# The last three rotations of the front and the first three local units in one hand-written order, with attention's buffers at the other end of SBUF

## The chip, the core and the metric

The kernel runs on one core of a Trainium2 chip. The metric is the device time of one execution in microseconds (us). One execution is also taken by the hardware profiler; the profile's times count from the first instruction of the program.

The engines are named as the profile names them: PE (TensorE, matmuls; PEld is its weight load), DVE (VectorE), ACT (ScalarE), POOL (GpSimd) and SP (SyncE, which here only issues DMAs). Each runs its own instructions in order, and they wait for each other by semaphores.

## The reference, cut to what matters

The input `x` is [16, 128, 128]: 16 samples of 128 tokens with 128 features. Two levels are computed; the change lies at the seam inside the first one.

```python
x = x + attn(cond(x))                    # level 0: conditioned 16-head causal attention
x = x + ffn(rigid_transform(x))          # level 0: each sample is rotated and moved as an image,
                                         #   then 6 layers of local attention + gated feed-forward
x = x + gated_linear_attention(laplace(x))   # level 1
x = x + moe(...)                             # level 1

def rigid_transform(X):   # per sample: bilinear samples of the 128x128 image at turned positions
    return sum of 4 gathers of X at (iy, ix), weighted by the distances

def local_layer(x):       # 6 times
    q, k, v = split(shift(x) @ Wqkv)                     # 16 heads of 64
    q, k = rotary(l2norm(q) * qs), rotary(l2norm(k) * ksc)
    x = softmax(band(q @ k.T)) @ v @ Wo + x
    return gated_gelu_ffn(layernorm(shift(x))) + x
```

## The kernel before, in words

**Stages.** `stage_front` does attention and rotation, `stage_local` the six local layers, `stage_tail` level 1. Inside a stage the order of PE, DVE, ACT and POOL is written out by hand: `run_step` walks a list such as `t.scores(0) w.rows(0) ...` and calls each piece in turn, and `manual_schedule` keeps that order on the four engines. SP's DMAs are placed by the tile framework's own scheduler. A letter stands for an object: `w` is the rotation (`Warp`) of one sample.

**The front.** `FRONT_STEP` is run for n = 0 to 18. In step n, attention of sample n begins (`t`), that of sample n-1 ends (`o`), and the rotation of sample n-3 is done (`w`). So step 16 ends attention of sample 15 and rotates sample 13; steps 17 and 18 only rotate samples 14 and 15. `o.write()` stores the attended sample as an image in DRAM, from which `gather` (POOL, eight indirect DMAs a sample) fetches boxes of pixels. A rotation then makes, on four quarters t: `far` (ACT, L479 and L486, distances), `hat` (DVE, L494, one SBUF tile clipped in place, two a quarter), `spread` (DVE, L455, `diag` from `box` and `own`, both in SBUF, two a sample), `rows` (PE, L502), `times` (DVE, L510, `prod` from PSUM and a hat), `sums` (PE, L520), and at the end `keep` (ACT, L527, and SP's `fr_moved` and `xs` DMAs), which puts the moved sample into `xs`.

**The local layers.** `Local` opens its pools after all of the front's pools are closed, so its weights lie over the front's buffers. `Layer(lo, 0)` loads `wqkv` (1536 KB), `wo` (512 KB), three pieces of `w2` (170 KB), `w1` (341 KB) and small tables; `prepare` makes `tab` (POOL, L673), `b1n` (PE L678, then DVE L684) and `w1n` (POOL, L686). Layer 1's weights are loaded right behind.

`STEP` is run for groups of four samples n = 0, 4, 8, ... In it `p0` to `p3` are the four new units: `project` (PE, L706, four a unit), `square` (ACT, L711), `cossin` (DVE, L719, `t`, four a unit), `sum_squares` (DVE, L729, two a unit), `rotate` (POOL, L743, four a unit), `lengths` (POOL, L735 and L736, the `pow`), `normalize_keys` (POOL, L748). `t0` to `t3` are units two behind, `o0` to `o3` three behind: `transpose` (PE, L770), `scores` (PE, L787), `mask` (DVE, L794), `maxima` (DVE, L801 and L806), `exponentials` (ACT, L814), `normalize` (POOL, L822), `turn`, `weigh`, `out`. So the group n = 0 has `p0` to `p3`, `t2` and `t3` (samples 0 and 1) and `o3` (sample 0) only. `f`, `e`, `g`, `h` are the feed-forward of earlier groups.

**The seam to the tail.** After the last feed-forward (`hT`, L941; `add`, DVE L955 into `xs`), `stage_local` turns the samples back on PE (L1019) and adds them to `xres` (DVE, L1025). `Tail` opens its pools over the local ones, clears `aT` (POOL, L1173), and `laplace` begins with `lx` (POOL, L1226; DVE, L1237), `diffuse` goes on with L1249, L1253 and L1256.

Of the kernel before, what the change touches and what calls it, by code (L numbers as in the profile page):

```python
# [15 lines left out]
P = 128  # L16
# [37 lines left out]
class Front:  # L54


    def __init__(self, s, ctx, xres):
        self.s, self.tc, self.nc, self.xres = s, s.tc, s.nc, xres
        tc, nc, a = s.tc, s.nc, s.a
        self.pools = {  # L60
            n: ctx.enter_context(tc.tile_pool(name=f"fr_{n}", bufs=n)) for n in (1, 2, 3, 4, 6)
        }
        self.sm = ctx.enter_context(tc.tile_pool(name="fr_sm", bufs=6))
        psum = lambda name, n: ctx.enter_context(
            tc.tile_pool(name=name, bufs=n, space=bass.MemoryType.PSUM)
        )
        self.rings = {"w": (psum("fr_w", 3), 1024), "g": (psum("fr_g", 2), 512)}
        self.n = 0
        self.image = [
            tc.dram_tile([P // 2, 13, 2, 32], F32, name=f"fr_image{b}") for b in range(B)  # L70
        ]
        self.moved = tc.dram_tile([B, P, 256], F32, name="fr_moved")
        wp = self.pools[1]
        by = lambda name, shape, src, eng=None: load(s, wp, name, shape, src, eng)


        self.tok = by("tok", [P, B], a["tok7"])
        self.wqk = [[None, None], [None, None]]
        for h in range(2):
            for k in range(2):  # L80
                self.wqk[k][h] = by(
                    f"wqk{k}{h}", [P, 512], a["a0_wqk"][k][:, 512 * h : 512 * h + 512], nc.scalar
                )
        self.cbias = by("cbias", [8, P], a["c0_bias"])

        self.xT = self.tile(1, "xT", [P, B, P])
        nc.sync.dma_start(out=self.xT[:, 0:4], in_=a["xT"][:, 0:4])
        self.bqk = by("bqk", [P, 2, 8], a["a0_bqk"])
        self.move = by("move", [P, 3, B], a["moves"])


        self.corner = by("corner", [P, 2, EIGHTS + QUADS], a["k_corner"])
        self.lane = by("lane", [P, 2], a["k_lane"])
        self.late = by("late", [P, 1024], a["k_late"])
        self.wv = by("wv", [P, 1024], a["a0_wv"], nc.scalar)
        nc.sync.dma_start(out=self.xT[:, 4:B], in_=a["xT"][:, 4:B])
        self.wo = by("wo", [P, 8, P], a["a0_wo"].rearrange("(c p) e -> p c e", p=P), nc.scalar)
        self.bv = by("bv", [P, 8], a["a0_bv"])
        self.bo = by("bo", [P, P], a["a0_bo"])
        nc.sync.dma_start(out=xres, in_=a["x"].rearrange("b t f -> t b f"))  # L100

        self.own = by("own", [P, 4], a["k_own"])
        self.sel = by("sel", [P, 44], a["k_quad"])

        self.eps = self.tile(1, "eps", [P, 1])
        nc.gpsimd.memset(self.eps, EPS_MASK)
        self.rem = self.tile(1, "rem", [P, 16])
        nc.gpsimd.iota(
            self.rem, pattern=[[1, 16]], base=0, channel_multiplier=0,
            allow_small_or_imprecise_dtypes=True,  # L110
        )
# [3 lines left out]

    def ps(self, ring):

        self.n += 1
        pool, cols = self.rings[ring]
        return pool.tile([P, cols], F32, tag=ring, name=f"{ring}{self.n}")  # L120

    def rows(self):

        nc, s = self.nc, self.s
        tokf = self.tile(1, "tokf", [P, B])
        nc.vector.tensor_copy(tokf, self.tok)
        self.row = self.tile(1, "rows", [P, B], U32)
        nc.vector.tensor_scalar(self.row, tokf, 128.0, s.pidx[:, 0:1], ALU.mult, ALU.add)
        self.onehot = self.tile(1, "onehot", [8, B])
        nc.vector.tensor_scalar(self.onehot, tokf[0:8], s.pidx[0:8, 0:1], None, ALU.is_equal)  # L130

    def lean(self):
        pb = self.ps("g")
        self.nc.tensor.matmul(pb[:, 0:B], self.cbias, self.onehot, start=True, stop=True)
        self.lean_of = self.tile(1, "lean", [P, B])
        self.nc.vector.tensor_copy(self.lean_of, pb[:, 0:B])
# [7 lines left out]
    def whole(self):  # L144


        pc = self.ps("g")
        for c in range(8):
            self.nc.tensor.matmul(
                pc[:, 0:P], self.bv[:, c : c + 1].to_broadcast([P, P]), self.wo[:, c, :],  # L150
                start=(c == 0), stop=(c == 7),
            )
        self.bias = self.tile(1, "bias", [P, P])
        self.nc.vector.tensor_tensor(self.bias, pc[:, 0:P], self.bo, ALU.add)
# [86 lines left out]
class Condition:  # L241
# [5 lines left out]
    def fetch(self):  # L247
        self.w = self.fr.tile(6, "wcond", [P, P])
        self.nc.gpsimd.indirect_dma_start(
            out=self.w, out_offset=None, in_=self.fr.s.a["c0_wT"],  # L250
            in_offset=bass.IndirectOffsetOnAxis(ap=self.fr.row[:, self.b : self.b + 1], axis=0),
            bounds_check=8 * P - 1,
        )

    def condition(self):
# [3 lines left out]
        if not self.pair:  # L259
            self.pair.append(self.fr.tile(3, "y", [P, 2, P]))  # L260
# [10 lines left out]
class Half:  # L271
# [17 lines left out]
    def keep(self, j):  # L289
        k, pr = j % 2, 4 * self.half + j // 2 * 2  # L290
        if k not in self.T:
            self.T[k] = self.fr.tile(2, f"qkT{k}", [P, 8, 256])
# [14 lines left out]
class FirstUnit:  # L307
# [14 lines left out]
    def keep_values(self, c):  # L322
        if c == 0:
            self.v = self.fr.tile(2, "v", [P, 1024])
# [27 lines left out]
    def exponentials(self, half):  # L352
        sc3 = self.sc[half].rearrange("p (h k) -> p h k", h=8)
        self.pe[half] = self.fr.tile(3, "pe", [P, 8, P])
# [19 lines left out]
    def keep_turn(self, i):  # L374
        self.pT[i] = self.fr.tile(4, "pT", [P, 4, P])
# [16 lines left out]
    def keep_weighed(self):  # L392
        self.oT = self.fr.tile(2, "oT", [P, 8, P])
# [177 lines left out]
def stage_front(s, xres):  # L571
# [3 lines left out]
    with ExitStack() as ctx:  # L575
        fr = Front(s, ctx, xres)
# [7 lines left out]
        engines = {e.engine for e in (nc.tensor, nc.vector, nc.scalar, nc.gpsimd)}  # L584
        with s.tc.manual_schedule(engines=engines):
# [5 lines left out]
            for n in range(B + 3):  # L591
                at = {k: v[n + d] for k, (v, d) in lists.items() if 0 <= n + d < B}
                run_step(FRONT_STEP, at)
# [15 lines left out]
class Local:  # L609


    def __init__(self, s, ctx):
        self.s, self.tc, self.nc, self.a = s, s.tc, s.nc, s.a
        nc = self.nc
        self.pools = {
            n: ctx.enter_context(s.tc.tile_pool(name=f"lo_{n}", bufs=n)) for n in (1, 2, 4, 6)
        }
        self.sm = ctx.enter_context(s.tc.tile_pool(name="lo_sm", bufs=6))
        psum = lambda name, n: ctx.enter_context(
            s.tc.tile_pool(name=name, bufs=n, space=bass.MemoryType.PSUM)  # L620
        )
        self.rings = {"s": (psum("lo_s", 2), 1024), "g": (psum("lo_g", 4), 512)}
        self.n = 0
# [4 lines left out]
        self.rot = load(s, self.pools[1], "rot", [P, 4, 64], self.a["k_rot"])  # L628
        self.band = load(s, self.pools[1], "band", [P, P], self.a["k_band"])
        self.mean = self.tile(1, "mean", [P, P])  # L630
        nc.vector.memset(self.mean, 1.0 / P)
        self.power = self.tile(1, "power", [P, 32])
        nc.vector.memset(self.power, -0.5)
        self.xs = s.xs
# [4 lines left out]
    def ps(self, ring):  # L639

        self.n += 1
# [9 lines left out]
class Layer:  # L651


    def __init__(self, lo, L):
        self.lo, self.number = lo, L
        s, nc, a, two, one = lo.s, lo.nc, lo.a, lo.pools[2], lo.pools[1]
# [4 lines left out]
        self.w2 = lo.tile(2, "w2", [P, 3, P])  # L661
# [8 lines left out]
    def prepare(self):  # L670
        lo, nc = self.lo, self.lo.nc
        self.tab = lo.tile(2, "tab", [P, 4, 64])
# [10 lines left out]
        self.b1 = lo.tile(2, "b1n", [P, 6])  # L683
        nc.vector.tensor_tensor(self.b1, pb[:, 0:6], self.rawb, ALU.add)  # L684
        self.w1 = lo.tile(2, "w1n", [P, 682])
# [3 lines left out]
class Unit:  # L689
# [18 lines left out]
    def square(self, k, c):  # L708
        if ("sq", k) not in self.bank:
            self.bank["sq", k] = self.lo.tile(2, "sq", [P, 1024])  # L710
# [4 lines left out]
    def cossin(self, k, c):  # L715

        if k not in self.t:
            self.t[k] = self.lo.tile(2, "t", [P, 2, 16, 64])
# [19 lines left out]
    def rotate(self, k):  # L738
        t = self.t[k]
        self.rot[k] = self.lo.tile(6, "rot", [P, 16, 64])  # L740
# [265 lines left out]
def stage_local(s, xres, early):  # L1006

    nc = s.nc
    with ExitStack() as ctx:
        lo = Local(s, ctx)  # L1010
        engines = {e.engine for e in (nc.tensor, nc.vector, nc.scalar, nc.gpsimd)}
        with s.tc.manual_schedule(engines=engines):
            run_layers(lo, early)

        for b0 in range(0, B, 4):
            pt = lo.ps("s")
            for i in range(4):
                for k, (rows, x) in enumerate(lo.halves(b0 + i, 1)):
                    nc.tensor.transpose(  # L1019
                        pt[:, 512 * k + 64 * i : 512 * k + 64 * i + 64],  # L1020
                        x.rearrange("p i t -> p (i t)"), s.ident[rows, rows],
                    )
            for k in range(2):
                xg = xres[:, b0 : b0 + 4, 64 * k : 64 * k + 64]
                nc.vector.tensor_tensor(  # L1025
                    xg, pt[:, 512 * k : 512 * k + 256].rearrange("p (i f) -> p i f", i=4), xg,
                    ALU.add,
                )


def run_layers(lo, early):
    total = DEPTH * B
    layers, units, ffs = [Layer(lo, 0)], {}, {}
    layers[0].prepare()
    for n in range(0, total + 12, 4):
        L, b = divmod(n, B)
        if n < total:
# [4 lines left out]
            for i in range(4):  # L1042
                units[n + i] = Unit(lo, layers[L], b + i)
# [6 lines left out]
        run_step(STEP, at)  # L1050
# [671 lines left out]
def tile_rec_block(ctx: ExitStack, tc: tile.TileContext, a: dict, out: bass.AP):  # L1722
# [5 lines left out]
    with tc.tile_pool(name="xs", bufs=1) as pool:  # L1728
# [4 lines left out]
        stage_front(s, xres)  # L1733
        stage_local(s, xres, early)
# [142 lines left out]
```

## Time and profile before

| | us |
|---|---|
| three runs, median (lowest to highest) | 2581.92 (2580.78 to 2582.80) |
| the profiled execution, its own time | 2586.6 |
| its span, first to last instruction | 2584.8 |
| PE busy in the span | 2432.3 (94%) |
| DVE busy | 2211.7 (86%) |
| ACT busy | 1924.3 (74%) |
| POOL busy | 1995.0 (77%) |

The stages, by the first or last instructions that mark them: the last copy L527 of front step 15 starts at 397.4, those of steps 16, 17 and 18 at 418.0, 434.5 and 447.9; the first local projection starts at 465.5, the second group's (n = 4) at 519.7, the third's (n = 8) at 588.2; a group in the middle takes 71.4. The tail runs from about 2258 to 2584.8.

How to read it: the page gives busy time of each engine and the chain of work that ended last; the windows view gives busy time, the granted TensorE clock (PEclk, 1.00 is full speed) and the DMA rate of any stretch; the timeline gives each instruction with its start, its length and, in brackets, how long its engine was idle before it and what ended that. Times come from one profiled execution.

### The profile page before, as it was taken

The page shows a single profiled execution, that of the slowest core. Times are in us where ns is not written, and L with a number is a line of the kernel's source. Part 1 is how long each engine was busy: PE and PEld are TensorE (multiplying, and loading weights), DVE is VectorE, ACT ScalarE, POOL GpSimd, SP SyncE. Part 2 cuts the span into 40 slices and gives each one's busy share as a digit, 9 for nine tenths or more (in the row PEclk, how much of TensorE's full clock was granted, in tenths as well). Part 3 has the DMA queues.
Part 4 walks back from the last instruction along what each step waited for, and adds up shares of the span by engine and source line. Part 5 has one row for each costly group of instructions (what it writes and reads, how often), then busy time and mean ns, then how long its engine had stood idle before and what let it go on. Part 6 is the DMA issues. An engine that isn't in the chain of part 4 may idle for free. (4 is left out here: it accounts for less than half of the span.)

```text
span 2584.8 us, 47593 instructions
## 1 busy us (share of the span) xinstructions
PE 2432.3 (94%) x17644; PEld 1677.5 (65%) x17644; DVE 2211.7 (86%) x2961; ACT 1924.3 (74%) x5717; POOL 1995.0 (77%) x1242
## 2 busy tenths in 40 slices
PE   7999997699999989999999999999999999789998
PEld 5676765366666666666666666666667666456666
DVE  5899997699999989999899989999899998454544
ACT  4788886488888878888788878888788888443422
POOL 3777675799999989999999999999999999243210
PEclk9999999799999999999999999999999999889999
DMA  3111111200001000100001000100000000021220
GB/s 107 29 30 33 29 29 39 80 1 5 13 5 38 8 8 5 38 8 5 13 5 38 8 7 7 38 8 5 6 5 5 5 3 4 17 64 64 93 70 25
DMA packets 89487, 64.73 MB, mean 25 GB/s; under 512 B 56802, under 2 KB 75944, under 8 KB 88488
## 3 DMA queue, kind: packets, MB, share of 16 engines
q1 hardware_dynamic: 78280, 37.56, 5.8%
q0 software_dynamic: 9216, 22.03, 2.8%
q8 instruction: 140, 2.29, 0.4%
q10 hardware_dynamic: 1760, 2.10, 0.3%
q14 instruction: 91, 0.75, 0.1%
HBM read 55.06 MB, written 6.60 MB: 24 GB/s over the span
## 5 line engine op out<-in xcount | busy, mean ns | idle before, releaser
L814 ACT ACTIVATE pe<-s,nm,r 128x128 f32<-128x128 f32 x1536 | 682.7, 486 | 2.3 <-DVE nm L806 1.7
L736 POOL TENSOR_TENSOR r<-ss,power 128x32 f32<-128x32 f32 x96 | 543.3, 5659 | 8.0
L719 DVE TENSOR_TENSOR t<-g,tab 128x1024 f32<-128x1024 f32 x384 | 461.8, 1216 | 48.2 <-PE g L706 32.1
L743 POOL TENSOR_TENSOR rot<-t 128x512 f32<-128x512 f32 x384 | 480.5, 1274 | 28.7 <-DVE t L719 28.6
L822 POOL TENSOR_TENSOR pe<-pe,den 128x1024 f32<-128x1024 f32 x192 | 363.5, 1898 | 40.0 <-DVE den L821 38.7
L706 PE MATMUL g<-wqkv,xs 128*128 128x512 f32 x768 | 393.4, 613 | 0.8 <-DVE t L719 0.4
L814 ACT ACTIVATION_READ_ACCUMULATOR pe<-s,nm,r 128x1 f32 x1536 | 359.3, 234 | 0.0
L711 ACT ACTIVATE sq<-g 128x512 f32<-128x512 f32 x384 | 230.8, 608 | 132.0 <-PE g L706 93.6
L775 ACT COPY qkT<-g 128x512 f32<-128x512 f32 x384 | 220.3, 615 | 56.4 <-PE g L770 55.7
L770 PEld LDWEIGHTS g<-ident,rot 128*128 128x128 f32 x1536 | 176.8, 144 | 115.5 <-issue 43.0
L770 PE MATMUL g<-ident,rot 128*128 128x128 f32 x1536 | 228.5, 282 | 23.6 <-ACT qkT L775 9.1
L794 DVE TENSOR_TENSOR s<-s,band 128x1024 f32<-128x1024 f32 x192 | 234.7, 1223 | 12.6 <-PE s L787 12.1
L828 PEld LDWEIGHTS g<-ident,pe 128*128 128x128 f32 x1536 | 179.3, 141 | 99.8 <-issue 87.9
L729 DVE TENSOR_REDUCE ss<-sq 128x16 f32<-128x1024 f32 x192 | 231.6, 1207 | 3.0 <-ACT sq L711 1.0
L801 DVE TENSOR_REDUCE nm<-s 128x8 f32<-128x1024 f32 x192 | 233.0, 1213 | 0.9
L787 PE MATMUL s<-qkT,qkT 64*128 64x128 f32 x3072 | 224.0, 285 | 5.5 <-ACT qkT L775 5.5
L787 PEld LDWEIGHTS s<-qkT,qkT 64*128 64x128 f32 x3072 | 187.2, 188 | 62.2 <-issue 51.1
L828 PE MATMUL g<-ident,pe 128*128 128x128 f32 x1536 | 222.6, 275 | 0.8 <-POOL pe L822 0.7
L835 DVE COPY pT<-g 128x512 f32<-128x512 f32 x288 | 192.7, 683 | 17.5 <-PE g L828 13.5
L842 PE MATMUL g<-pT,v 128*64 128x128 f32 x3072 | 200.6, 278 | 2.0 <-DVE pT L835 2.0
L755 PE MATMUL g<-wqkv,xs 128*128 128x512 f32 x384 | 202.2, 608 | 0.0
L842 PEld LDWEIGHTS g<-pT,v 128*64 128x64 f32 x3072 | 165.4, 137 | 50.6 <-DVE nm L801 18.2
(333 smaller groups left out, 4784.5 us busy)
## 6 DMA issues: line engine op xcount, KB each, us to landing
wqkv<-in_lo_wqkv_dram SPq DMA_DIRECT2D x6, 1536.0 KB
roots<-lo_roots SPq DMA_DIRECT2D x24, 256.0 KB
fr_image<-xres SPq DMA_DIRECT2D x32, 104.0 KB
wo<-in_lo_wo_dram SPq DMA_DIRECT2D x6, 512.0 KB
box<-fr_image,idx POOLq DMA_INDIRECT x128
fr_moved<-out SPq DMA_DIRECT2D x16, 128.0 KB
w<-in_lo_w_dram SPq DMA_DIRECT2D x6, 341.0 KB
wqk<-in_a_wqk_dram ACTq DMA_DIRECT2D x4, 256.0 KB
```

Of the source, the lines that this page charges most:

```text
L706: self.nc.tensor.matmul(pq, self.xT, self.w.qkv[:, at : at + 512], start=True, stop=True)
L719: self.nc.vector.tensor_tensor(self.t[k][:, :, 8 * c : 8 * c + 8, :], heads(self.bank["q", k, c]).unsqueeze(1).to_broadcast([P, 2, 8, 64]) ...
L736: self.nc.gpsimd.tensor_tensor(self.r, self.ss, self.lo.power, ALU.pow)
L743: self.nc.gpsimd.tensor_tensor(self.rot[k][:, :, at], t[:, 0, :, at], t[:, 1, :, other], ALU.add)
L770: self.nc.tensor.transpose(pt[:, j * P : j * P + P], flat[:, at : at + P], self.s.ident)
L787: self.nc.tensor.matmul(sc[:, k * 512 + j * P : k * 512 + j * P + P], self.T[0][rows, pr, :], self.T[1][rows, pr, :], start=True, stop=True,)
L794: self.nc.vector.tensor_tensor(sc, sc, self.lo.band.unsqueeze(1).to_broadcast([P, 8, P]), ALU.add)
L801: nc.vector.tensor_reduce(nm, self.sc[half].rearrange("p (h k) -> p h k", h=8), AX.X, ALU.max, negate=True)
L814: self.nc.scalar.activation(self.pe[half][:, h, :], sc3[:, h, :], AF.Exp, bias=self.nm[half][:, h : h + 1], scale=self.r[:, hd : hd + 1], ...
L822: self.nc.gpsimd.tensor_tensor(pe, pe, den.unsqueeze(2).to_broadcast([P, 8, P]), ALU.mult)
L828: self.nc.tensor.transpose(pt[:, j * P : j * P + P], self.pe[i // 2][:, 4 * (i % 2) + j, :], self.s.ident)
L842: self.nc.tensor.matmul(po[rows, j * P : (j + 1) * P], self.v[:, hd * 64 : hd * 64 + 64], self.pT[2 * half + k][:, j, :], start=True, stop ...
```

## The change

1. **Two sides of SBUF.** Attention's buffers (its weights, `xT`, `y`, `qkT`, `v`, `pe`, `pT`, `oT`, small ones) go into pools `at_*` on the right end; what the rotations need stays in `fr_*` on the left. The `at_*` pools are closed after step 16's `o.write()`, by `FRONT_LAST`, which is `FRONT_STEP` cut there.
2. **Local's weights and the p-units' tiles on the right.** `Local` opens `2w`, `1w`, `2p`, `6p` and `lo_sm` on the right as soon as attention's pools are closed, with `reuse_waits="tile"`: a tile waits for the tiles that lay at its addresses. The rest (`lo_1`, `lo_2`, `lo_4`, PSUM) is opened by `open()` once the front's pools are closed.
3. **One order for the seam.** `lo.begin()` loads layer 0's weights and runs `prepare`; then `BLEND` holds the rest of step 16 (`u`, sample 13), steps 17 and 18 (`v`, `w`, samples 14 and 15) and the units `p0`, `p1`, `p2`. Their projections take PSUM from the front's ring `w` (three buffers of two banks), half of a buffer each. `FIRST` takes the place of `STEP` for n = 0, without `p0` to `p2`.

```diff
 class Front:
-    def __init__(self, s, ctx, xres):
+    def __init__(self, s, ctx, ctx_at, xres):
+        self.at_pools = {
+            n: ctx_at.enter_context(tc.tile_pool(name=f"at_{n}", bufs=n, side="right"))
+            for n in (1, 2, 3, 4, 6)
+        }
...
+FRONT_LAST = FRONT_STEP[: FRONT_STEP.index("o.write()") + 1]
+BLEND = """
+u.rows(3) v.hat(0,0) v.far(0,1) u.times(2) v.gather(3) v.spread(0) u.sums(1) v.far(1,0)
+u.times(3) v.hat(1,0) v.rows(0) u.sums(2) v.far(0,2) v.hat(0,1) v.hat(0,2) v.rows(1) v.times(0)
+v.far(1,1) w.bases() v.hat(1,1) v.spread(1) v.far(0,3) p0.project(0,0) v.sums(0) v.far(1,2)
+v.hat(1,2) v.rows(2) v.times(1) w.far(0,0) p0.square(0,0) u.sums(3) p0.project(1,0) v.hat(0,3)
+p0.cossin(0,0) v.far(1,3) w.far(1,0) v.hat(1,3) v.times(2) p0.project(0,1) v.rows(3) w.gather(0)
...
+w.sums(3) p1.lengths() p2.cossin(0,0) p1.normalize_keys() w.keep() p2.square(0,1)
+p2.sum_squares(0) p2.cossin(0,1) p2.rotate(1) p2.rotate(0) p2.lengths() p2.normalize_keys()
+""".split()
...
-            for n in range(B + 3):
+            for n in range(B + 1):
                 at = {k: v[n + d] for k, (v, d) in lists.items() if 0 <= n + d < B}
-                run_step(FRONT_STEP, at)
+                run_step(FRONT_STEP if n < B else FRONT_LAST, at)
+    lo = Local(s, ctx_local, fr)
+    with s.tc.manual_schedule(engines=engines):
+        lo.begin()
+        at = dict(zip("uvw", warps[B - 3 :]))
+        run_step(BLEND, {**at, **{f"p{i}": lo.units[i] for i in range(3)}})
+    return lo
...
 class Local:
+    def begin(self):
+        s, nc = self.s, self.nc
+        self.layers.append(Layer(self, 0))
...
+        self.layers[0].prepare()
+        for b in range(4):
+            self.units[b] = Unit(self, self.layers[0], b)
+
+    def open(self):
+        pool = lambda name, n, **kw: self.ctx.enter_context(
+            self.s.tc.tile_pool(name=name, bufs=n, reuse_waits="tile", **kw)
+        )
+        for n in (1, 2, 4):
+            self.pools[n] = pool(f"lo_{n}", n)
...
     def ps(self, ring):
+        if self.rings is None:
+            return self.front.ps("w")[:, 0:512]
...
+FIRST = """
+t2.transpose(1,0) t2.transpose(0,0) t2.values(0) t2.keep_transpose(0,0) t2.keep_transpose(1,0)
...
+t3.normalize(1) p3.lengths() p3.normalize_keys()
+""".split()
...
-        run_step(STEP, at)
+        run_step(STEP if n else FIRST, at)
...
-        stage_front(s, xres)
-        stage_local(s, xres, early)
+        with ExitStack() as local:
+            with ExitStack() as front:
+                lo = stage_front(s, xres, front, local)
+            stage_local(s, lo, xres, early)
```

In the changed kernel as it is built, `prepare` is the first work after step 16's `o.write()` on PE, DVE and POOL, ahead of all of `BLEND`; on SP the load of `wqkv` waits for the last matmul of sample 15's `o.out()` and stands ahead of that sample's image; layer 1's loads stand directly behind layer 0's. From the group n = 4 to the last local group the four engines' orders are those of before. At the seam to the tail, DVE and POOL have `lx` of the first two tail groups ahead of the last feed-forward's `add` and of the clearing of `aT`.

## The prediction

> **What bounds the kernel now.** I read the page first. Its chain that ended last covers only the tail, so it says nothing of the seam between front and local layers. I therefore asked for busy time by stage (length, then busy us of PE, PEld, DVE, ACT, POOL, granted clock, DMA share, GB/s):
>
> ```profile
> 397.40:418.00 20.60, 17.79 (x160) 13.07 (x160) 15.90 (x19) 13.12 (x27) 16.18 (x14) 0.92 0.21 37
> 418.00:434.50 16.50, 11.54 (x96) 8.66 (x96) 13.95 (x15) 12.02 (x26) 10.69 (x10) 0.90 0.13 27
> 434.50:448.00 13.50, 9.86 (x96) 7.17 (x96) 11.09 (x13) 8.87 (x20) 0.00 (x0) 1.00 0.08 16
> 448.00:465.50 17.50, 2.25 (x12) 2.28 (x13) 0.27 (x3) 0.30 (x1) 2.75 (x2) 0.61 0.85 275
> 465.50:519.70 54.20, 40.83 (x206) 23.99 (x206) 42.68 (x45) 29.51 (x90) 45.89 (x27) 0.81 0.08 22
> 662.50:734.00 71.50, 70.79 (x526) 48.38 (x525) 67.57 (x83) 60.01 (x184) 66.82 (x38) 1.00 0.05 12
> ```
>
> The last line is the steady local layer: PE 70.8 of 71.5, so PE sets the pace and whatever is won before it stays won. At the seam nothing is full. From 397.4 to 519.7 are 122.3 us, in which DVE, the busiest, has 83.9 of work: at most 38 us can be won. The 17.5 us from 448.0 are a stop of all engines while DMA moves 275 GB/s. The timeline there shows the chain:
>
> ```profile
> 409.40 2.05 PE L399 MATMUL g<-wo,oT 128*128 128x128 f32 x16 [0.52 <-ACT oT L394]
> ...
> 453.14 0.55 SPq L1060 DMA_DIRECT2D wqkv<-in_lo_wqkv_dram  x1
> ...
> 462.65 2.02 POOL L686 TENSOR_SCALAR w1n<-w,gbb 128x682 f32<-128x682 f32 x1 [8.74 <-DMA gbb<-in_lo_gbb_dram]
> 463.25 2.41 PE L678 MATMUL g<-gbb,w 128*128 128x1 f32 x12 [15.40 <-DMA gbb<-in_lo_gbb_dram]
> 465.75 0.17 DVE L684 TENSOR_TENSOR b1n<-g,b 128x6 f32<-128x6 f32 x1 [17.32 <-PE g L678]
> ```
>
> The weights' load, then `prepare`, then the first projection. The first `cossin` is at 467.7; DVE stood from 448.3.
>
> **A. The load is moved, and its wait with it.** Now `wqkv` waits for the end of L399 (411.45); I take its issue at 411.9, where before the image store was issued. But `prepare` stands ahead of `BLEND` on PE (L678), DVE (`b1n`) and POOL (`tab`, `w1n`), so these three wait for `w1`, `gbb`, `scl` and `rot`; behind them wait all rotations, and POOL's gathers of samples 14 and 15. Before, 9.5 us passed from the issue of `wqkv` to `w1n`, with 2218 KB (`wqkv`, `wo`, `w2`) ahead of `gbb`. Now `w1` (341 KB) and the image (208 KB) are ahead too: 549 KB at 275 GB/s, 2.0 us. So L678 starts at 411.9 + 11.5 = 423.4 and DVE is free 2.41 + 0.17 + 0.1 later, at 426.1. Bounds: 9.5 us (424.1) and twice that, as the small loads on SP now each wait for an earlier landing (433.6). DVE, which reaches `b1n` at 413.5, stands 12.6 us where it stood 19.4. Layer 1's loads follow on SP and share the DMA engines with the gathers; POOL is free at about 427, two gathers, `bases` (2.7) and eight gathers of 1.24 + 0.3 end near 445, and the first `diag` of sample 15 comes after 448 on DVE: covered by 3 us.
>
> **B. BLEND is bound by DVE.** Between `b1n` and the first local `mask`, DVE has 16 hats, 10 `prod`, 4 `diag`, 12 `t` and 6 `ss`. The first three are what it did from 413.4 to 448.3 (groups view, DVE in that stretch: count, busy, mean ns, idle before):
>
> ```profile
> L510 DVE TENSOR_TENSOR prod<-w,hat 128x1024 f32<-128x1024 f32 x10 | 12.2, 1221 | 4.8 <-PE w L502 4.7
> L494 DVE TENSOR_SCALAR hat<-hat 128x1024 f32<-128x1024 f32 x16 | 11.0, 725 | 1.0 <-ACT hat L486 0.9
> L455 DVE TENSOR_TENSOR diag<-box,own 128x1024 f32<-128x1024 f32 x4 | 6.3, 1580 | 0.0
> ```
>
> 29.5 us, plus 12 x 1.217 (`t`) = 14.6 and 6 x 1.208 (`ss`) = 7.2: 51.3, and 0.7 of spacing (front step 15 had DVE busy 24.56 of 24.90). PE has 25.5 (its busy time in that stretch) and 12 projections of 0.6 to 1.2, under 40; ACT 22.8 + 12 x 0.6; both have room. The 4.8 us that DVE idled for L502 now hold p-work. POOL has 38 us for p0 to p2 (12.7 each: 4 x 1.27, 0.29, 5.46, 1.91); it starts at about 445 and lags DVE by the last `lengths`, as before. I add 1.0 for PE at half clock after its stop (projections of 1.20 instead of 0.59 at 465.5) and for three PSUM buffers shared by `rows` and projections; bounds 0 and 6 (0.5 for each of 12 projections).
>
> **C. DVE beside POOL.** What is new is hats and diags beside POOL's rotations. Timeline, DVE and POOL:
>
> ```profile
> 396.74 0.64 DVE L494 TENSOR_SCALAR hat<-hat 128x1024 f32<-128x1024 f32 x1
> 396.97 2.16 POOL L365 TENSOR_TENSOR pe<-pe,den 128x1024 f32<-128x1024 f32 x1
> 397.30 2.92 DVE L455 TENSOR_TENSOR diag<-box,own 128x1024 f32<-128x1024 f32 x1
> ...
> 608.50 6.37 POOL L736 TENSOR_TENSOR r<-ss,power 128x32 f32<-128x32 f32 x1
> 608.50 1.09 DVE L917 TENSOR_TENSOR xn<-roots,xc 128x512 f32<-128x512 f32 x1
> ```
>
> A `diag` takes 1.21 alone and 2.92 beside a POOL tensor operation, 1.7 more; hats, at best 0.68, go to 2.4 there. `prod` and `t`, which read PSUM, keep 1.22 beside everything. Beside the `pow`, L917 with two SBUF inputs keeps 1.09, so I let only rotations and key scalings block. Behind p0's first rotation stand 8 hats and 2 diags; POOL rotates or scales for about 16 of those 33 us, so every second one waits about 1 us: 5.0. Bounds 0 and 10 x 1.7 = 17.
>
> [...]
>
> So the first `mask` comes at 426.1 + 52.0 + 1.0 + 5.0 = 484.1, where it was at 490.9: 6.8 won. The one late transfer there, ACT's first `keep_transpose` waiting for sample 15's `fr_moved` to land (2.4 us at most before), starts some 10 us earlier and hides.
>
> **D. FIRST.** From the first `mask` to the next group's first projection were 28.8 us (490.9 to 519.7). Out of that stretch go two `t` and two `ss` of p2, 4.9 us of DVE: 23.9. POOL needs 10 us after the mask for p2's end, then four normalizings (7.6) and p3 (12.7), to 514, where that scaling of p3 ended at 531.6. The group n = 4 so begins at 508.0: 11.7 won.
>
> **E. Catching up.** In that group PE idled 0.67 us for POOL at 546 and 2.0 for DVE at 549. POOL is now 17 us earlier, so most of it goes: 2.0 (bounds 0 and 2.7).
>
> **F. The tail's start.** The new buffers free `lx` from the last `add`:
>
> ```profile
> 2260.41 1.95 POOL L1173 MEMSET aT<- 128x512 f32 x4
> ...
> 2262.34 1.02 POOL L1226 TENSOR_TENSOR lx<-xres 128x504 f32<-128x504 f32 x1
> ...
> 2263.39 1.09 DVE L1237 SCALAR_TENSOR_TENSOR lx<-xres,lx 128x512 f32<-128x512 f32 x1 [2.42 <-POOL lx L1226]
> ```
>
> L1253 came at 2264.7 behind this. Now both `lx` run from 2253.5 on, and L1253 waits for ACT (2263.3): 1.3 won. Against it the last `add` moves behind them by some 1.4, but L1025 behind it stood after L1237 already. Bounds -0.5 and 1.4.
>
> **The sum.** 11.7 + 2.0 + 1.3 = 15.0. The profiled execution took 2586.6 (span 2584.8 and 1.8 around it): 2571.6. The median of the runs is 4.7 below it, so 2566.9; I say 2567.
>
> **Rivals.** *More than that* (12%): no blocking (5.0), loads in 9.5 us (2.0), all of E (0.7): 22.7 won, 2559. For it: hats beside gathers, the other POOL work, cost 0.1 only.
>
> *The wait only moves* (15%): loads take 19 us (7.5 lost) and each projection waits half a us for its PSUM buffer (5 more): 2.5 won, 2579. For it: `prepare` heads the blend on three engines, so the early load hides behind almost nothing. Against: the build shows no wait of `wqkv` later than L399, and 19 us would be 145 GB/s.
>
> *Slower* (7%): blocking hits all 20 hats and diags at the worst row, 1.7 each, 34 us against my 5: 14 lost, 2596. It decides from 1.0 us an operation (20 us in all, no gain). Against: POOL holds its operands half of the time, and half of these stand before its first rotation.
>
> *As summed* (66%), 10 to 20 won.
>
> The range reaches from 2560 (nearly all of the first rival) to 2577 (half of the second). Same means within 0.2%, 5.2 us, about what a measurement of this kernel can tell. Faster by more: the sum, the first rival and half of the second, 0.85; same 0.09; slower 0.06.
>
> **What would show it.** Right: `wqkv` issued near 412, L678 idle some 9 us and starting at 422 to 425; no stop of all engines after; DVE busy over 90% from 426 to the first `mask` near 484; hats beside POOL's rotations of over 1 us; the group n = 4's first projection near 508; the first L1253 some 1.3 us sooner after the last `hT`. Wrong: L678 after 430, DVE idling for PE or POOL inside the blend by over 5 us in all, hats waiting beside the pow, or a steady group longer than 71.5.

## The result and the profile after

| | median of the runs, us | ratio to before, 95% interval | profiled execution, us (span) |
|---|---|---|---|
| before | 2582.36 (2580.78 to 2583.23) | | 2586.6 (2584.8) |
| changed | 2564.16 (2563.86 to 2565.58) | 0.9931 [0.9914, 0.9948] | 2565.58 (2563.5) |

18.2 us faster, where 15.0 were forecast and 2560 to 2577 was the range. Lines have moved with the change: L771 is `project`, L743 the matmuls of `prepare`, L749 `b1n`, L502 `hat`, L463 `diag`, L518 `prod`, L784 `t`, L801 the `pow`, L808 `rotate`, L835 `transpose`, L859 `mask`, L893 and L907 `turn` and `weigh`.

I count the seam from the end of the front's last output matmul (L399 before, L407 now) to the first projection of the group n = 4: 411.45 to 519.7, **108.2 us** before, and 409.53 to 497.9, **88.4 us** now. Busy time by stage after (length, then busy us of PE, PEld, DVE, ACT, POOL, granted clock, DMA share, GB/s), the cuts being `b1n`'s start, the first `mask`, and the groups n = 4 and n = 8:

```profile
409.50:423.90 14.40, 5.03 (x39) 4.10 (x39) 2.68 (x9) 4.15 (x8) 1.58 (x2) 0.73 0.90 256
423.90:477.30 53.40, 45.31 (x291) 24.97 (x292) 49.54 (x49) 29.19 (x60) 49.97 (x32) 0.88 0.22 61
477.30:497.90 20.60, 18.47 (x147) 12.69 (x148) 19.84 (x23) 19.32 (x71) 18.00 (x11) 1.00 0.02 2
497.90:566.70 68.80, 64.34 (x500) 44.65 (x499) 64.25 (x81) 57.25 (x189) 65.66 (x36) 0.98 0.00 1
```

The first line is the old stop, now shorter and at another place: 14.4 us with 2.7 of DVE work, and DMA at 256 GB/s. The second is the blend, with DVE busy for 49.5 of 53.4. The timeline of the first stretch, SP, PE, DVE and POOL:

```profile
409.60 0.34 SPq L1142 DMA_DIRECT2D wqkv<-in_lo_wqkv_dram  x1
...
418.46 0.43 SPq L1142 DMA_DIRECT2D gbb<-in_lo_gbb_dram  x1
...
421.40 2.41 PE L743 MATMUL w<-gbb,w 128*128 128x1 f32 x12 [9.37 <-DMA gbb<-in_lo_gbb_dram]
...
423.84 0.17 DVE L749 TENSOR_TENSOR b1n<-w,b 128x6 f32<-128x6 f32 x1 [11.71 <-PE w L743]
...
424.01 1.18 POOL L738 TENSOR_TENSOR tab<-rot,scl 128x256 f32<-128x256 f32 x1 [12.62 <-DMA rot<-in_k_rot_dram]
```

`wqkv` is issued at once, `gbb` 8.9 us behind it in SP's queue (L1142 is the helper that issues a load), and PE, DVE and POOL stand for 9 to 13 us each.

The two profiled executions differ by 21.3 us of span, 3 more than the medians. 1.9 of these lie ahead of the seam, where the work and its order are the same: in the kernel before, a `rows` group of front step 16 took 3.28 us instead of 2.00, at a granted clock of 0.59 instead of 1.00 (windows 400.20 to 403.60 before, 400.50 to 402.60 after), as the two timelines show (before, then after):

```profile
400.27 3.28 PE L502 MATMUL w<-hat,diag 64*128 64x256 f32 x16 [1.33 <-DVE diag L455]
```
```profile
400.57 2.00 PE L510 MATMUL w<-hat,diag 64*128 64x256 f32 x16 [1.32 <-DVE diag L463]
```

Two profiles of the changed kernel differ too: from the first `mask` to n = 4 the granted clock was 1.00 in one and 0.92 in the other (e9), whose seam was 90.8. So below the seam is read from the profile, the gain from the times, and a seam is good to some 2 us.

### The profile page after: what moved, and what is told of

Read it like the earlier page. It is cut to its first block, busy times and chain, and to the rows that moved or that the text cites. A ratio compares the mean times of both kernels' runs of the same rounds, so it can differ in the third digit from the quotient of the medians.

```text
span 2563.5 us, 47591 instructions
## 1 busy us (share of the span) xinstructions
PE 2431.5 (95%) x17644; PEld 1673.8 (65%) x17644; DVE 2209.3 (86%) x2961; ACT 1924.3 (75%) x5717; POOL 1993.5 (78%) x1242
## 4 chain that ended last, share of the span: by engine, by line
PE 55%; DVE 11%; ACT 6%; issue 1%; POOL 1%; DMA 1%; DVEq 0%; POOLq 0%; ACTq 0%; SPq 0%
PE g L771 9%; PE s L852 6%; PE g L835 5%; PE g L907 5%; PE g L990 5%; PE g L820 4%; PE g L893 4%; PE g L923 4%; ACT pe L879 3%; DVE t L784 2%; DVE nm L866 2%; PE e L1527 2%; DVE ss L794 1%; PE o L1545 1%; DVE nm L871 1%
## 5 line engine op out<-in xcount | busy, mean ns | idle before, releaser
L801 POOL TENSOR_TENSOR r<-ss,power 128x32 f32<-128x32 f32 x96 | 541.0, 5635 | 8.0
L808 POOL TENSOR_TENSOR rot<-t 128x512 f32<-128x512 f32 x384 | 481.8, 1276 | 20.7 <-DVE t L784 20.6
L784 DVE TENSOR_TENSOR t<-g,tab 128x1024 f32<-128x1024 f32 x372 | 447.5, 1217 | 43.6 <-PE g L771 32.4
L771 PE MATMUL g<-wqkv,xs 128*128 128x512 f32 x744 | 380.7, 610 | 0.6 <-DVE t L784 0.4
L776 ACT ACTIVATE sq<-g 128x512 f32<-128x512 f32 x372 | 223.8, 609 | 95.7 <-PE g L771 86.8
L859 DVE TENSOR_TENSOR s<-s,band 128x1024 f32<-128x1024 f32 x192 | 234.7, 1222 | 12.6 <-PE s L852 12.1
L835 PEld LDWEIGHTS g<-ident,rot 128*128 128x128 f32 x1536 | 174.6, 142 | 106.6 <-issue 43.4
L893 PEld LDWEIGHTS g<-ident,pe 128*128 128x128 f32 x1536 | 179.6, 141 | 98.4 <-issue 87.4
L835 PE MATMUL g<-ident,rot 128*128 128x128 f32 x1536 | 226.3, 281 | 16.5 <-ACT qkT L840 8.7
L852 PE MATMUL s<-qkT,qkT 64*128 64x128 f32 x3072 | 223.1, 285 | 3.8 <-ACT pe L879 1.9
L852 PEld LDWEIGHTS s<-qkT,qkT 64*128 64x128 f32 x3072 | 186.3, 187 | 61.7 <-issue 51.5
L893 PE MATMUL g<-ident,pe 128*128 128x128 f32 x1536 | 222.9, 276 | 1.3 <-POOL pe L887 0.9
L820 PE MATMUL g<-wqkv,xs 128*128 128x512 f32 x384 | 202.3, 609 | 0.0
L907 PE MATMUL g<-pT,v 128*64 128x128 f32 x3072 | 199.9, 277 | 0.8 <-DVE pT L900 0.8
L923 PEld LDWEIGHTS g<-oT,wo 128*128 128x128 f32 x1536 | 182.7, 192 | 22.9 <-issue 16.7
```

Source lines behind the costliest of these rows:

```text
L771: self.nc.tensor.matmul(pq, self.xT, self.w.qkv[:, at : at + 512], start=True, stop=True)
L784: self.nc.vector.tensor_tensor(self.t[k][:, :, 8 * c : 8 * c + 8, :], heads(self.bank["q", k, c]).unsqueeze(1).to_broadcast([P, 2, 8, 64]) ...
L801: self.nc.gpsimd.tensor_tensor(self.r, self.ss, self.lo.power, ALU.pow)
L808: self.nc.gpsimd.tensor_tensor(self.rot[k][:, :, at], t[:, 0, :, at], t[:, 1, :, other], ALU.add)
L820: self.nc.tensor.matmul(pv, self.xT, self.w.qkv[:, 2048 + c * 512 : 2560 + c * 512], start=True, stop=True)
L835: self.nc.tensor.transpose(pt[:, j * P : j * P + P], flat[:, at : at + P], self.s.ident)
```

## Experiments

Each kernel is the changed one with the edit shown. "Seam" is as defined above, from one profiled execution each; the ratio is to the kernel before, timed on the same chip as the run (medians of 2579.7 to 2581.1 us there).

| run | median, us | ratio to before, 95% | seam, us |
|---|---|---|---|
| e9, changed kernel again | 2563.07 | 0.9935 [0.9921, 0.9948] | 90.8 |
| e4, no interleaving, `prepare` first | 2581.65 | 1.0006 [0.9996, 1.0015] | 108.3 |
| e3, no interleaving, `prepare` late | 2572.76 | 0.9965 [0.9949, 0.9980] | 102.0 |
| e5, before's group order, early load | 2570.88 | 0.9963 [0.9952, 0.9974] | 99.2 |
| e6, first group in STEP's order | 2568.34 | 0.9952 [0.9937, 0.9967] | 93.2 |
| e2, small loads first | 2564.23 | 0.9940 [0.9923, 0.9956] | 85.5 |
| e1, `prepare` late | 2555.82 | 0.9905 [0.9889, 0.9922] | 84.7 |
| e7, both | 2554.91 | 0.9906 [0.9891, 0.9921] | 80.7 |
| e8, both, layer 1 loaded by ACT | 2561.82 | 0.9923 [0.9909, 0.9937] | 78.9 |
| e10, `prepare` late, table's loads first | **2552.52** | **0.9892 [0.9877, 0.9907]** | 79.4 |
| e11, e10 and two of layer 1's loads by ACT | 2552.34 | 0.9891 [0.9876, 0.9907] | 79.1 |

**What the parts of the change are worth: e3 to e6.** e3 and e4 take the interleaving out:

```diff
-BLEND (u, v, w and p0..p2 mixed; prepare() in begin())
+e3: all of u, v, w in BLEND's order, then prepare(), then p0..p2 in BLEND's order
+e4: prepare(), then all of u, v, w, then p0..p2
```

> The changed kernel without the interleaving: the same operations, the early load kept, but first all of samples 13 to 15, then `prepare`, then the three local units. Theory 'the early load is what pays': DVE has 35 us from 412 to about 447 with the load hidden under it, then 22 of p-work as in the kernel before, first `mask` 23 us after at about 470 and the group n = 4 at 491 to 497: the time of the changed kernel or up to 6 us less (2558 to 2565). Rival 'the interleaving is what pays' (the gaps of one chain hold the work of the other): p0 to p2 alone run with DVE idle for PE, ACT and POOL as before, the group n = 4 at 503 or later and 5 to 10 us more than the changed kernel (2569 to 2574).

> As the run with the order undone, but with `prepare` at the head, where the changed kernel has it: the load's wait is exposed again. Against the run with `prepare` behind samples 13 to 15 it must lose the exposed wait, about 11.8 us, by the theory that the wait is only moved (2570 to 2577), and 2 us or less by the rival that transfers collide in any case. Against the changed kernel it differs by the interleaving alone: 6 to 12 us more by my sum, none by the theory that the early load is all.

e3 came out at 2572.8 with the group n = 4 at 508.8: the rival's numbers, not mine. e4 lost 8.9 us to e3 (6.3 of seam) where 11.8 were expected, and came out at 2581.7 where 2570 to 2577 were; it lost some 18 to the changed kernel, where I had 6 to 12. But both runs do more than undo the interleaving: all of `p0` to `p2` now stands ahead of the transposes of sample 0, which the old STEP had between them. From the first `cossin` to the first `mask` e3 took 33.0 us, the kernel before 23.3. So e5 keeps the old STEP for the first group:

```diff
-BLEND (mixed); STEP if n else FIRST
+all of u, v, w in BLEND's order, then prepare(); STEP for every n
```

> The changed kernel's buffers and early load, but the kernel before's order: first all of samples 13 to 15, then `prepare`, then the first group in the old STEP, in which the transposes of sample 0 stand among the projections of samples 1 and 2. The seam is counted from the end of the front's last output matmul (L407) to the first projection of the group n = 4: 108.2 us in the kernel before, 88.4 in the changed one. Theory 'load and interleaving each pay a part': the stop of 19.4 us for the load goes, less some 6 us by which samples 13 to 15 ran later in the runs with the loads beside them: a seam of 95 to 99, time some 9 to 13 us less than before. Rival 'the early load alone pays nothing' (as the run with `prepare` at the head and no interleaving suggests, whose seam was 108.3): a seam of 104 or more. Rival 'it pays all': 90 or less.

```profile
408.30:455.50 47.20, 36.71 (x272) 23.59 (x272) 30.29 (x39) 24.20 (x51) 18.19 (x16) 0.79 0.52 142
455.50:478.50 23.00, 14.68 (x51) 7.45 (x50) 16.38 (x14) 7.78 (x14) 19.79 (x13) 0.75 0.06 12
478.50:507.50 29.00, 23.74 (x153) 15.37 (x154) 26.33 (x30) 21.83 (x77) 26.17 (x15) 0.88 0.00 1
```

In these stages of e5 (to the first `cossin`, to the first `mask`, to n = 4) the last two take 52.0 us as before (52.0 from 467.7), and the whole gain is in the first, 47.2 instead of 56.3. A seam of 99.2 and 2570.9 us, at the edge of what the theory of two parts gave (95 to 99): the early load in the old order is worth 9 us, and the rest of the 19.8 is the order.

e6 undoes the new order FIRST alone:

```diff
-        run_step(STEP if n else FIRST, at)
+        run_step(STEP if n else [x for x in STEP if x in FIRST], at)
```

> The changed kernel with the first group's remaining operations in the order of the old STEP instead of the new order FIRST. From the first `mask` to the group n = 4 the changed kernel took 20.6 us where I had 23.9. Theory 'the new order of the first group is worth the 3.3 us': 23 to 25 us from `mask` to the group, and 2 to 4 us more time in all. Rival 'TensorE's clock is worth it' (0.88 granted in that stretch before, 1.00 in the changed kernel): 20 to 21.5 us, the time of the changed kernel.

```profile
477.20:502.60 25.40, 20.68 (x149) 14.33 (x150) 20.03 (x26) 20.71 (x74) 17.99 (x11) 0.93 0.02 3
```

With the same operations, `mask` to n = 4 takes 25.4 us instead of 20.6, DVE being as busy (20.0 against 19.8): a difference of 4.8 us in the profile and 4.2 to 5.3 in the medians, a little more than the theory's 2 to 4. The clock may have a part in it, since the changed kernel itself took 22.6 us there in e9, at a granted clock of 0.92 instead of 1.00:

```profile
477.10:499.70 22.60, 19.80 (x146) 13.89 (x147) 21.85 (x25) 19.71 (x71) 17.12 (x10) 0.92 0.02 3
```

So FIRST explains at least 2.8 of it. Going from e5 to e6 (99.2 to 93.2) is the blend, 6.0, net of the load's wait, which e5 hides and e6 doesn't. The 19.8 us of the seam are thus about 9 of early load, 6 of interleaving with its exposed wait, and 5 of FIRST, up to 2 of which may be the clock; each is good to some 2 us.

**Whether the wait was only moved: e1, e2, e7, e10.** `prepare` is cut in two, and both halves go behind rotation work:

```diff
-        self.layers[0].prepare()               # in begin(): tab, then L743, b1n, w1n
+BLEND: ... v.hat(0,3) q.tables() p0.cossin(0,0) ... w.gather(1) q.fold() p0.rotate(0) ...
+        # tables(): tab on POOL; fold(): L743, b1n, w1n
```

> The changed kernel, but `prepare` is cut in two and put into the blend: the table (POOL) just before the first `cossin`, the matmuls L743 with `b1n` and `w1n` after the last gather. Theory 'the wait was only moved to where nothing covers it': in the changed kernel DVE, PE and POOL all stood from about 412 to 423.9 for the weights' load; here the rest of samples 13 to 15 runs under it. DVE has about 13 us of work ahead of the first `cossin`, so nearly all of the 11.8 us goes: the blend's first hat at 412, the first `mask` at 466 to 469 instead of 477.3, time 8 to 11 us less than the changed kernel (2553 to 2556). Rival 'the transfers collide': samples 14 and 15 are gathered while 2.6 MB of weights pass, their boxes land late, `diag` waits for them and POOL, which had 50.0 of the 53.4 us of the blend, sets the end: 0 to 4 us less (2560 to 2564).

By the ratios (0.9905 against e9's 0.9935) 7.7 us less than the changed kernel, a little under the theory's 8 to 11. The first `mask` comes at 468.9, within the expected 466 to 469, but 2.7 us of that lie ahead of the seam (L407 ends at 406.8 instead of 409.5), and the seam is only 3.7 us shorter (6.1 against e9's). The timeline of e1 has new waits, on DVE and then on POOL (L740 is `tab` there):

```profile
413.49 1.23 DVE L463 TENSOR_TENSOR diag<-box,own 128x1024 f32<-128x1024 f32 x1 [1.69 <-DMA box<-fr_image,idx]
```
```profile
420.30 0.79 POOL L740 TENSOR_TENSOR tab<-rot,scl 128x256 f32<-128x256 f32 x1 [7.46 <-DMA rot<-in_k_rot_dram]
```

POOL stands for the table, whose `rot` is last but one in SP's queue, and the eight gathers of sample 15 stand behind it. The other way is to bring the small loads first:

```diff
-wqkv, wo, w2, w1, b1, gbb, scl, rot, band
+w1, b1, gbb, scl, rot, wqkv, wo, w2, band
```

> The changed kernel with another order of layer 0's loads alone: `w1`, `b1`, `gbb`, `scl` and `rot` (some 0.7 MB) ahead of `wqkv`, `wo` and `w2`; `prepare` still heads the blend. Theory 'the wait was only moved': L743 starts 4 to 6 us after the first load is issued instead of 11.8, and the first projection, which is 9.7 us behind `b1n`, does not wait for `wqkv`; 6 to 8 us less than the changed kernel (2556 to 2558). Rival 'a fixed delay of the small loads' (many small descriptors, each waiting for an earlier landing, and not the 2.2 MB ahead of them): L743 after 420 still, less than 2 us won.

The matmuls of `prepare` (L743, L749 in e2) now start 5.0 us after L407's end instead of 11.9, which excludes the rival's 420. The edit did more than reorder, though: `w1` is issued at 399.2, 7.1 us ahead of L407's end, and `wqkv` only 4.7 us after it, behind the image store. Counted from the first issue, as the theory counted, those matmuls come after 12.1 us and not after 4 to 6. The seam wins 2.9 us only, and the median of the runs (2564.2, with one run, the profiled one, at 2557.7) shows no gain where 6 to 8 us were expected: as a time e2 is inconclusive. The reason for the small seam is in DVE's timeline:

```profile
426.78 1.22 DVE L463 TENSOR_TENSOR diag<-box,own 128x1024 f32<-128x1024 f32 x1 [4.10 <-DMA box<-fr_image,idx]
```

POOL still heads the blend with `tab` and `w1n`, so the last two gathers of sample 14 are issued only at 418.8 and 420.4, and DVE has their box at 426.8. e7 makes both edits:

> Both edits together: `prepare` cut in two and put late, and the small loads of layer 0 ahead of the large ones. With `prepare` late alone POOL stood 7.5 us for `rot`, and sample 15's gathers, behind it, began at 421; with the small loads first DVE stood 4.1 us for a box of sample 14, whose gathers POOL issued only at 419. Theory 'each edit ends on the other's wait': together the table is ready near 414, no engine stands for a load, the seam is 78 to 81 us (84.7 and 85.5 for the single edits), time 2549 to 2553. Rival 'the transfers themselves collide' (layer 1's 2.2 MB follow at once on the same DMA engines, and the boxes land behind them): 83 to 85, no better than `prepare` late alone.

The seam fell to 80.7, as the theory said; the time, 2554.9, is 2 above its range and not told from e1's. What is left of the waits for loads is POOL's for `rot`, 2.5 us, and PE's for `wqkv`, now behind 0.6 MB of small loads (L782 is `project` there):

```profile
421.99 1.43 PE L782 MATMUL w<-wqkv,xs 128*128 128x512 f32 x2 [2.45 <-DMA wqkv<-in_lo_wqkv_dram]
```

So e10 puts only what the table needs ahead of `wqkv`:

```diff
-wqkv, wo, w2, w1, b1, gbb, scl, rot, band
+scl, rot, wqkv, wo, w2, w1, b1, gbb, band      # and prepare cut in two, as in e1
```

> The changed kernel itself, on the same chip as the last two, so that they can be compared with it without the spread between chips and clocks: 2562 to 2566, a seam of 88 to 89 us.

> `prepare` cut in two and put late, and of layer 0's loads only `scl` and `rot`, which the table needs (0.26 MB), ahead of `wqkv`; `w1`, `b1` and `gbb` stay last, since the late matmuls L743 need them some 20 us later. With all small loads first PE stood 2.45 us for `wqkv` and DVE some 3 us behind it. Theory 'the rest of the wait was the order of the loads': no wait for `rot` over 3 us on POOL and none for `wqkv` on PE, a seam of 78 to 80 us (80.7 with all small loads first, 88.4 in the changed kernel), 8 to 10 us less time than the changed kernel. Rival 'the clock at half speed after the stop sets that stretch': a seam of 80 to 82.

```profile
407.40:423.00 15.60, 13.49 (x123) 8.89 (x122) 15.60 (x21) 13.83 (x29) 13.46 (x12) 1.00 0.84 234
423.00:464.10 41.10, 32.22 (x213) 17.88 (x206) 35.57 (x37) 19.59 (x40) 39.06 (x23) 0.96 0.28 78
464.10:486.80 22.70, 19.80 (x147) 13.85 (x148) 21.93 (x25) 19.76 (x72) 17.15 (x10) 0.92 0.02 2
```

The first line is to be held against the changed kernel's 409.50 to 423.90: DVE is busy for all of the 15.6 us, beside 234 GB/s of loads, and PE's granted clock is 1.00. 2552.5 us against 2563.1 for the changed kernel on the same chip: 10.5 us less, with intervals that don't touch. It is the fastest version here together with e11, and 28.6 us below the 2581.14 of before. Of the 11.8 us in which the changed kernel stood for the weights, 9.0 of seam are won (11.4 against e9). Against e1 the order of the loads wins 5.3 us of seam; as a time it is not shown, since the intervals of e1, e7 and e10 overlap. As in e2, the first load (`scl`) goes out before L407's end, at 401.0, and `wqkv` 4.0 us after it.

**Whether transfers collide: e8, e11.** Layer 1's loads follow layer 0's at once on SP. e8, on top of e7, takes all nine away and lets ACT issue them in the group n = 8; e11 does so with `wqkv` and `wo` only, on top of e10:

```diff
+        eng = nc.scalar if L == 1 else nc.sync
-        nc.sync.dma_start(out=self.w2[0:n, c, :], ...)      # and the other eight
+        eng.dma_start(out=self.w2[0:n, c, :], ...)
```

> As both edits together, and layer 1's nine loads are issued by ACT in the third group (n = 8) instead of by SP right behind layer 0's, so that no transfer but layer 0's weights is beside the gathers of samples 14 and 15. Theory 'the transfers collide': 2 to 5 us less than with both edits alone, DVE without a wait for a box. Rival 'they do not': the same seam within 1 us, and perhaps 0 to 2 us more for ACT's issues in the group n = 8.

> As the run with the table's loads first, and of layer 1's loads only `wqkv` and `wo` (the first two of nine, which found a free queue) are issued by ACT in the group n = 8. With all nine there, ACT stood 7.3 us for an earlier landing and that group took 85.0 us instead of 74.3. Theory 'ACT stands only where a later load on its queue waits for an earlier one': the group n = 8 is back to 74 to 75 us, and the seam is that of the run with the table's loads first or up to 2 us less. Rival 'any load on ACT's queue holds ACT until it has landed': a group n = 8 of 80 us or more.

The seams, 78.9 against 80.7 (e7) and 79.1 against 79.4 (e10), differ by no more than two profiles of one kernel: layer 1's transfers cost the blend nothing that these runs could show. What e8 did show is the price of ACT's queue. Its time is 6.9 us above e7's, where the theory had 2 to 5 less and the rival up to 2 more, and its n = 8 group took 85.0 us instead of 74.3 (L730 and L1154 issue loads there, L852 is `keep_transpose`):

```profile
553.67 3.35 ACTq L730 DMA_DIRECT2D w<-in_lo_w_dram  x3
...
559.27 0.34 ACTq L1154 DMA_DIRECT2D gbb<-in_lo_gbb_dram  x1
561.14 0.33 ACTq L1154 DMA_DIRECT2D scl<-in_lo_scale_dram  x1
561.52 1.07 ACT L852 COPY qkT<-g 128x512 f32<-128x512 f32 x2 [7.30 <-DMA w<-in_lo_w_dram]
```

By the bracket, ACT's stop ends with the landing of an earlier load: the later issues wait for it, and ACT's copies stand behind them for 7.3 us. With the first two loads alone (e11) that group is back at 74.3, which is the theory stated for e11.

## Why the prediction was right, and where its terms were off

The direction, the mechanism (load, blend and order each give a part, DVE paces the blend) and the range held; the terms of the sum did not all.

**A, the load's wait moves with the load: right.** From L407's end `b1n` was to be done after 14.65 us (426.1 less 411.45) and was done after 14.5; 11.5 us from `wqkv`'s issue to L743 were 11.8. That this wait was not covered, the core of the rival "the wait only moves", is shown by e10, which covers it and is 10.5 us faster. The rival's price was wrong: the load took 11.8 us, not 19, and of the projections one waited for its PSUM buffer, for 0.2 us (467.68, for `prod`).

**B and C, the blend: bound by DVE as argued, C over-sized.** From `b1n` to the first `mask` I had 58.0 us, measured were 53.4. POOL was as busy there as DVE (50.0 and 49.5 us), but none of DVE's waits is for POOL. The groups view of DVE in the blend, to be read against the rows shown for before:

```profile
L784 DVE TENSOR_TENSOR t<-w,tab 128x1024 f32<-128x1024 f32 x12 | 14.3, 1212 | 1.2 <-ACT sq L776 1.2
L502 DVE TENSOR_SCALAR hat<-hat 128x1024 f32<-128x1024 f32 x16 | 12.9, 829 | 0.0
L518 DVE TENSOR_TENSOR prod<-w,hat 128x1024 f32<-128x1024 f32 x10 | 12.1, 1214 | 0.9 <-PE w L510 0.9
L794 DVE TENSOR_REDUCE ss<-sq 128x16 f32<-128x1024 f32 x6 | 7.1, 1204 | 0.0
L463 DVE TENSOR_TENSOR diag<-box,own 128x1024 f32<-128x1024 f32 x4 | 5.8, 1438 | 0.0
```

These busy times add up to 52.2 us, near B's 51.3, yet DVE was busy for 49.5 in all, because neighbours overlap (below, the hats begin 1.15 us after a `diag` of 1.22). B added 0.7 for spacing where 2.7 come off, and had 1.0 for waits where DVE idled for 3.9: its 53.0 came out near right because two errors cancel.

C is the term that was too dear. Hats rose by 1.9 us (11.0 to 12.9) and diags fell by 0.5: 1.4 net, where C put 5.0 by letting every second of ten operations wait 1 us. What C meant to price, POOL's work for the p-units, cost one hat (1.24 instead of 0.68, at 445.90) and one `diag` (1.89 instead of 1.21), 1.2 us together. The rest stands beside `base` on POOL, as in the old order: three hats at 428.71 took 3.36 us (three took 1.89 elsewhere in the kernel before, first line below; L476 is `base`), and before it was one `diag` of 2.68 at 418.27. The timeline shows why few waited (DVE before; then DVE and POOL after; L813 is `normalize_keys`):

```profile
442.30 1.89 DVE L494 TENSOR_SCALAR hat<-hat 128x1024 f32<-128x1024 f32 x3
```
```profile
428.71 3.36 DVE L502 TENSOR_SCALAR hat<-hat 128x1024 f32<-128x1024 f32 x3
...
445.90 1.24 DVE L502 TENSOR_SCALAR hat<-hat 128x1024 f32<-128x1024 f32 x1
447.06 1.22 DVE L463 TENSOR_TENSOR diag<-box,own 128x1024 f32<-128x1024 f32 x1
448.21 1.34 DVE L502 TENSOR_SCALAR hat<-hat 128x1024 f32<-128x1024 f32 x2
...
453.39 0.68 DVE L502 TENSOR_SCALAR hat<-hat 128x1024 f32<-128x1024 f32 x1
...
457.61 1.89 DVE L463 TENSOR_TENSOR diag<-box,own 128x1024 f32<-128x1024 f32 x1
```
```profile
430.30 1.20 POOL L476 TENSOR_TENSOR base<-add,add 128x256 f32<-128x256 f32 x2
...
444.08 2.49 POOL L808 TENSOR_TENSOR rot<-t 128x512 f32<-128x512 f32 x2
...
447.38 6.76 POOL L801 TENSOR_TENSOR r<-ss,power 128x32 f32<-128x32 f32 x1
...
456.51 1.90 POOL L813 TENSOR_TENSOR rot<-rot,r 128x1024 f32<-128x1024 f32 x1
458.37 6.95 POOL L808 TENSOR_TENSOR rot<-t 128x512 f32<-128x512 f32 x4
...
466.64 5.46 POOL L801 TENSOR_TENSOR r<-ss,power 128x32 f32<-128x32 f32 x1
...
474.04 4.97 POOL L808 TENSOR_TENSOR rot<-t 128x512 f32<-128x512 f32 x4
```

One `diag`, at 457.61 beside a key scaling and a rotation on POOL, still took 1.89 us instead of 1.21. But four rotations beside hats and a diag took 6.95 us instead of 4.97: there POOL took 2.0 us longer, and no wait of DVE in the blend came of it. And three hats inside the `pow` took some 0.7 each, their time alone; it had begun before them (447.38), and took 6.76 us instead of 5.46 (6.25 in e10, with the same three hats inside). Only this one of the blend's pows met hats.

**D, the first group: a term put at nothing.** "Out of that stretch go two `t` and two `ss`" took the old order's time for granted: 23.9 us from `mask` to n = 4, measured 20.6. e6 shows that in the old order the same work takes 25.4, so my 23.9 was, if anything, short for that order; I had costed what FIRST leaves out and nothing for how it is ordered, which is worth 2.8 to 4.8 us.

**E, catching up in n = 4: nothing.** I expected POOL's 17 us of head start to remove 2.0 us of PE's waits there; the group took 68.8 us against 68.5. The timelines (PE, before and after) have the same two waits at the same distance from the group's start, 26.7 to 29.8 us before and 27.0 to 30.1 after:

```profile
546.40 0.66 PE L828 MATMUL g<-ident,pe 128*128 128x128 f32 x4 [0.67 <-POOL pe L822]
549.51 0.63 PE L770 MATMUL g<-ident,rot 128*128 128x128 f32 x4 [2.01 <-DVE t L719]
```
```profile
524.91 0.66 PE L893 MATMUL g<-ident,pe 128*128 128x128 f32 x4 [0.67 <-POOL pe L887]
528.02 0.63 PE L835 MATMUL g<-ident,rot 128*128 128x128 f32 x4 [2.02 <-DVE t L784]
```

The head start itself was not there. I compared POOL's times (514 against 531.6) without the group's own move. The last work on POOL for `p3` (before, then after) ends 11.9 us after the group's start before (531.6 against 519.7) and 12.2 after (510.1 against 497.9):

```profile
529.72 1.90 POOL L748 TENSOR_TENSOR rot<-rot,r 128x1024 f32<-128x1024 f32 x1
```
```profile
508.20 1.90 POOL L813 TENSOR_TENSOR rot<-rot,r 128x1024 f32<-128x1024 f32 x1
```

Whether a POOL that is really ahead would shorten these waits, no run shows.

**F, the tail's start: given back.** Timeline of DVE at the end of the last layer, after (L1319 is `lx`, L1020 the last `add`, L1108 the addition to `xres`; L1331, L1335 and L1349 were L1249, L1253 and L1267):

```profile
2237.65 0.92 DVE L1319 SCALAR_TENSOR_TENSOR lx<-xres,lx 128x512 f32<-128x512 f32 x1
2238.49 0.34 DVE L1331 SCALAR_TENSOR_TENSOR e<-xres,z,e 128x128 f32<-128x128 f32 x1
2238.75 1.52 DVE L1020 SCALAR_TENSOR_TENSOR xs<-g,gbb,xs 64x512 f32<-64x512 f32 x2
...
2244.56 0.35 DVE L1335 SCALAR_TENSOR_TENSOR c<-lx,z,c 128x128 f32<-128x128 f32 x1 [2.75 <-ACT c L1328]
...
2250.26 0.69 DVE L1349 COPY cT<-g 128x512 f32<-128x512 f32 x1
```

Counted from the last down-projection (2234.21 now, 2253.51 before) the first L1335 comes 0.8 us sooner (10.35 against 11.16), but `cT` (L1349) at 16.05 against 15.97. The last `add`, L1020, now stands behind both `lx` on DVE and runs 1.7 us later (4.54 after that matmul, 2.88 before), and through L1108 and PE the matmul that ACT waits for comes later too; the second L1335 (2246.14) waits for ACT once more. The lower end of my bounds had this, the value taken did not. It is read from the traces; no run isolates it.

The sum by measured terms is 19.8 for the seam (11.7 forecast), -0.3 for E and -0.1 for F: 19.4 in the profile, 18.2 in the medians. So the seam won 8.1 us more than forecast (0.2 in A, 4.6 in the blend, mostly C, and 3.3 in D), while the 3.3 us of E and F did not come (0.4 were lost there). That the total lies within 3.2 us of the forecast is partly luck: errors of both signs cancel.

## What to carry to other kernels

A load that is issued early hides little until the first instruction that needs it also stands behind other work, on every engine that has one: here moving `prepare` and two small loads was worth another 10.5 us, 7.7 of them with `prepare` alone (e1). Order the loads of one queue by first use, and put only what is needed first ahead of the big one: that won 5.3 us of seam here (e10 against e1), and with all small loads ahead PE stood 2.45 us for `wqkv` (e7). Undo an ordering by restoring the old order whole: a cut that keeps half of the new one (e3, e4) measured its own bad order.

## What the runs showed of the hardware

- Three DVE hats within POOL's `pow` took some 0.7 us each, as alone, and the `pow` took 6.76 us instead of 5.46 (6.25 in e10).
- PE's granted clock fell to half in its stop: by the windows view it was 1.00 from 412.1 to 416.1, 0.50 from 416.3 to 428.4 and 1.00 again from 430.0. The first `rows` group behind the load (423.74) took 3.78 us instead of 2.00. When the clock was 1.00 again, PE had worked since 421.40 without a stop, some 8.5 us.
- Nine DMA issues on ACT's queue cost ACT 7.3 us in one stop (e8), two cost nothing that shows (e11).
